# A Mamba scan with its carried state folded into the drive term, and time-step rows fetched in two parts

## Chip, cores and metric

One core of one Trainium2 chip. The metric is the device time of one execution in microseconds; three runs before the change gave 7946.76, 7952.61 and 7958.2, median 7952.61 us. The engines are named as in the profile: PE (TensorE), DVE (VectorE), ACT (ScalarE), POOL (GpSimd) and SP (SyncE, which here only issues DMAs).

## What is computed

Two layers with skips, on x of shape (4, 512, 64, 64): x = x + mamba_layer(group_norm(x)), then x = x + linear_attention(group_norm(x)). The change lies in the scan of the first layer. The 512 channels of each of the four images are cut into 4 chunks of 128; each chunk goes through the same Mamba block with 256 inner channels and 16 states, over a sequence of 4096 positions:

```python
dt = softplus(dbc[..., :8] @ dt_proj_w.T + dt_proj_b)
A = -jnp.exp(A_log)
def step(h, inp):
    dt_t, B_t, C_t, x_t = inp
    dA = jnp.exp(dt_t[:, :, None] * A)
    h = dA * h + (dt_t * x_t)[:, :, None] * B_t[:, None, :]
    y = jnp.einsum('bds,bs->bd', h, C_t)
    return (h, y)
_, ys = lax.scan(step, h0, ...)
y = (ys + xc * D_param) * silu(z)
```

Below, u is dt * x (here x is the block's convolved input), "drive" is u * B, and the state h at the end of one tile of positions is the start of the next tile.

## The kernel before

**Tiles and steps.** The 4096 positions are cut into 8 tiles of T = 512. A *step* is one (image b, tile t, chunk c), c innermost: 4 x 8 x 4 = 128 steps. So the same chunk's next tile comes four steps later, and its state waits in `st`. A step has 16 *slots*, numbered s = 0 to 15 (g counts slots over the whole loop, 2048 in all): two halves of the inner channels (e), in each four groups of states (q), in each two slots (jj) of two scans. So a step has 32 scans of 128x512. Partitions hold 4 states by 32 channels. Two slots, a *pair*, share one tile `h` of 128x4x512.

**What a slot does** (`slot`, lines 725 to 754):

- `drive(g + 2)` on POOL: the product of u and B, 128x1024, into a tile `bx` (three buffers), line 721;
- in even slots `b_row`, in odd slots `c_tail`: four small DMAs each, on SP's queue, that spread rows of B or of the last quarter of C over the partitions (line 688);
- two scans on DVE, line 739, each with `decay` for the scan three further on: ACT's exponential into one of three PSUM banks `dA` (line 713). A scan starts from the constant 0.0 in tile 0 and from a column of `st` in tiles 1 to 7;
- in even slots, between the two scans, DVE's product of the pair before with C's first 384 positions (`product`, line 759); `fold_states` follows it on PE (the sum over states into `y`);
- in odd slots, after the second scan, POOL's copy of the four last columns of `h` into `st` (line 750) and POOL's product of the last 128 positions with C, the *tail* (line 751).

PE's fold of a pair needs the tail; it frees one of the two `h` buffers for the pair after the next one.

**Between slots** the function `after` places the rest by slot number. That part is written out by hand, and each engine runs its instructions in the order written; the framework adds only the waits on data and buffers. What matters here: dt of the next step is made in slot 3 by ACT (two Softplus, line 620, with a table load before and after); in slot 4 POOL makes u next to it (line 628; the tile `both`, 128x2x2x512, tag `dt`, has one buffer); in slot 5 SP writes both to DRAM (line 631, one DMA each); in slot 9 SP fetches both back for the next step's first half, each over four groups of partitions: eight DMAs of 256 KB (`spread`, line 639). The second half is fetched in slot 1 of the step itself, eight DMAs again. Gates (POOL, line 781) come in slots 1 and 9, Silu with two table loads (ACT) in slot 10.

**Attention and the norms** of other tiles run in the same slots, mainly on PE and ACT, from the end of batch 0 on. After the last scan (7493.4 us into the span) the last image's attention runs alone.

**SP's queue** has all loads and stores of the loop, in order. An issue waits until the DMA issued eight places earlier has landed: over the trace no issue starts before that landing, and a fifth of them start within 0.2 us after it.

Of the kernel before, what the change touches and what calls it, by code (L numbers as in the profile page):

```python
# [24 lines left out]
def kernel(  # L25
# [196 lines left out]


    w_cv = const.tile([P, NTAP, DI], F32, tag="w_cv", name="w_cv")
    w_x = wk.tile([P, DI], F32, tag="bx", name="w_x", bufs=3)
    nc.scalar.dma_start(w_x, in_w[:, 0:DI])
    conv_bc = wk.tile([P, NTAP, DI], F32, tag="h", name="conv_bc", bufs=2)
    nc.scalar.dma_start(conv_bc, conv_w.partition_broadcast(P))
# [41 lines left out]


    bqk = const.tile([P, C], BF16, tag="bqk", name="bqk")
    b_qk = wk.tile([P, C], F32, tag="bx", name="b_qk", bufs=3)
    nc.vector.memset(b_qk, 0.0)
    for i in range(P // LANE):
        nc.scalar.dma_start(
# [290 lines left out]
    def shifted_end(f, name):  # L567
        mv = small.tile([P, NC, 2], F32, tag="mv", name=f"mv_{name}", bufs=4)
        for v in range(2):
            nc.vector.tensor_reduce(mv[:, :, v], f[("sum", "square")[v]], AX.X, ALU.add)  # L570
        nc.vector.tensor_scalar(mv, mv, 1.0 / L, None, ALU.mult)
        d2 = small.tile([P, NC], F32, tag="d2", name=f"d2_{name}")
        nc.vector.tensor_tensor(d2, mv[:, :, 0], mv[:, :, 0], ALU.mult)
        nc.vector.tensor_tensor(mv[:, :, 1], mv[:, :, 1], d2, ALU.subtract)
        nc.vector.tensor_tensor(mv[:, :, 0], mv[:, :, 0], f["mv"][:, :, 0], ALU.add)
        return mv
# [41 lines left out]
    def time_steps(f, nm):  # L618
        for e in range(NH):
            nc.scalar.activation(  # L620
                f["both"][:, 0, e, :], f["pt"][e], AF.Softplus, bias=dtb[:, e : e + 1]
            )

    def to_rows(f, v, nm):

        both = f["both"]
        if v:
            nc.gpsimd.tensor_tensor(f["both"][:, 1], f["both"][:, 0], f["xz"][:, 0], ALU.mult)  # L628
        d_rows = dram.tile([P, NH, T], F32, tag=f"d_rows{v}", name=f"d_rows{v}_{nm}")
        f["d_rows", v] = d_rows  # L630
        later(1, lambda: nc.sync.dma_start(d_rows, both[:, v]))

    def spread(f, e, nm):

        d = wk.tile([P, 2, NJ, T], F32, tag="d_all", name=f"d_all_{nm}_{e}")
        for v in range(2):
            src = f["d_rows", v].rearrange("(j i) e t -> i e j t", i=BLK)[:, e]
            for k in range(KS):
                nc.sync.dma_start(d[k * BLK : (k + 1) * BLK, v], src)  # L639
        f["d_all", e] = d  # L640

    def mixers(f, nm):

        pd = work_bank(f"pd_{nm}", 0)
        for e in range(NH):
            mm(pd, w_xp[:, e, :], f["xz"][:, 0, e, :], start=(e == 0), stop=(e == NH - 1))
        yield
        f["both"] = wk.tile([P, 2, NH, T], F32, tag="dt", name=f"dt_{nm}", bufs=1)  # L650
        dtr = f["dtr"] = f["both"][0 : 2 * LANE, 1, NH - 1, :]
# [28 lines left out]
        e, r = divmod(r, NQ * JJ)  # L680
        return n, e, *divmod(r, JJ)

    b_all, c_all, c_sb, dAs, bxs, hs, ys = {}, {}, {}, {}, {}, {}, {}

    def for_states(dst, rows_, q):

# [30 lines left out]
    def drive(g):  # L717

        n, e, q, jj = place(g)
        bxs[g] = wk.tile([P, 2, T], F32, tag="bx", name=f"bx_{g}", bufs=3)  # L720
        nc.gpsimd.tensor_tensor(  # L721
            bxs[g], fs[n]["d_all", e][:, 1, jj * 2 : jj * 2 + 2, :], bc(b_all[g // JJ], 2), ALU.mult
        )

    def slot(g, last, after):
        n, e, q, jj = place(g)
        b, t, c = steps[n]
        if g + 2 < last:
            drive(g + 2)
        if jj == 0:  # L730
            if g + 3 * JJ < last:
                b_row(g + 3 * JJ)
            hs[g // JJ] = wk.tile([P, NJ, T], F32, tag="h", name=f"h_{g}", bufs=2)
        elif g + 1 < last:
            c_tail(g + 1)
        h = hs[g // JJ]
        for i in range(2):
            j = jj * 2 + i
            nc.vector.tensor_tensor_scan(  # L739
                h[:, j, :], dAs.pop(2 * g + i), bxs[g][:, i, :],  # L740
                0.0 if t == 0 else st[:, c, e, q, j : j + 1], ALU.mult, ALU.add,
            )
# [5 lines left out]
        del bxs[g]  # L748
        if jj == JJ - 1:
            nc.gpsimd.tensor_copy(st[:, c, e, q, :], h[:, :, T - 1])  # L750
            nc.gpsimd.tensor_tensor(  # L751
                h[:, :, CUT:], h[:, :, CUT:], bc(c_sb.pop(g // JJ), NJ), ALU.mult
            )
# [52 lines left out]
    def attention(b, x1s, stats):  # L806
# [87 lines left out]

        kqn = wk.tile([P, NC, P], F32, tag="res", name=f"kqn_{b}", bufs=2)
        nc.gpsimd.memset(kqn, 0.0)
        nrm = small.tile([P, NC], F32, tag="nrm", name=f"nrm_{b}")
# [116 lines left out]
    def run(pieces):  # L1014
        for _ in pieces:
            pass
# [59 lines left out]
    c_tail(0)  # L1076
    time_banks(fs[0], names[0])
    time_steps(fs[0], names[0])
    for v in range(2):
        to_rows(fs[0], v, names[0])  # L1080
    spread(fs[0], 0, names[0])
    for g in range(JJ, 3 * JJ, JJ):
        b_row(g)
    c_row(0)
    for g in range(2):
        drive(g)
    run(step_inputs(1))
    silu(1)
    run(mixers(fs[1], names[1]))
# [4 lines left out]
    with tc.manual_schedule():  # L1094
        credit, seen, mix, held[0], held_x[0] = 0.0, work["mm"], iter(()), 0, 0
        for n, (b, t, c) in enumerate(steps):
# [10 lines left out]
            for s in range(SLOTS):  # L1107
                def after():
# [8 lines left out]
                        take_y(f, n, 0)  # L1117
                    if s < 2:
                        next(last_mix, None)
                    if s == 1:  # L1120
                        spread(f, 1, nm)
                        if before is not None:
                            gate(before, 1)
                    if s == 2 and nxt is not None:
                        time_banks(nxt, names[n + 1])
                    if s == 3 and nxt is not None:
# [7 lines left out]
                            add_to(late, leave(pb_, pt_))  # L1134
                    if s in (3, 5, 6, 7, 8, 9):
                        next(front, None)
                    if s == 4 and nxt is not None:
                        to_rows(nxt, 0, names[n + 1])
                        to_rows(nxt, 1, names[n + 1])
                    if s == 4 and before is not None:  # L1140
                        pb_, pt_, pc_ = steps[n - 1]
                        out_proj(before, xn[pb_, pt_], pc_, names[n - 1])
                    if s == 9:
                        gate(f, 0)
                        if nxt is not None:
                            spread(nxt, 0, names[n + 1])
                    if s == 10 and n + 2 < N:
                        silu(n + 2)
                        nc.scalar.preload_act_table_set("natural_log_exp_and_others")
# [90 lines left out]
```

## Time and profile before

| | |
|---|---|
| median of 3 runs | 7952.61 us |
| profiled execution | 7963.09 us, its span 7961.4 us |
| mean granted TensorE clock | 0.897 |
| busy: DVE, POOL | 6977.7 (88%), 6880.5 (86%) us |
| busy: PE, ACT | 6453.6 (81%), 5507.6 (69%) us |
| DMA | 1265.87 MB, mean 159 GB/s |
| loop of scans | 122.4 to 7493.4 us of the span |
| POOL copies into `st` | 1024, mean 204 ns, median 188 ns, 209.1 us busy |
| `d_all` fetches, `d_rows` writes, median to landing | 6.7 us (256 KB), 3.6 us (512 KB) |

Busy time is the union of an engine's instructions; an engine idles where it waits for another. A group of instructions is one line, engine and pair of tiles: its count, its busy time, the mean of one, and the idle time of the engine just before them with what ended most of it. Records of consecutive independent instructions overlap by some 0.05 us on POOL and 0.08 on DVE, so distances between starts tell throughput better than durations.

### The profile page before, as it was taken

The page shows a single profiled execution, that of the slowest core. Times are in us where ns is not written, and L with a number is a line of the kernel's source. Part 1 is how long each engine was busy: PE and PEld are TensorE (multiplying, and loading weights), DVE is VectorE, ACT ScalarE, POOL GpSimd, SP SyncE. Part 2 cuts the span into 40 slices and gives each one's busy share as a digit, 9 for nine tenths or more (in the row PEclk, how much of TensorE's full clock was granted, in tenths as well). Part 3 has the DMA queues.
Part 4 walks back from the last instruction along what each step waited for, and adds up shares of the span by engine and source line. Part 5 has one row for each costly group of instructions (what it writes and reads, how often), then busy time and mean ns, then how long its engine had stood idle before and what let it go on. Part 6 is the DMA issues. An engine that isn't in the chain of part 4 may idle for free.

```text
span 7961.4 us, 90563 instructions
## 1 busy us (share of the span) xinstructions
PE 6453.6 (81%) x24835; PEld 2120.0 (27%) x24880; DVE 6977.7 (88%) x5766; ACT 5507.6 (69%) x8321; POOL 6880.5 (86%) x4597
## 2 busy tenths in 40 slices
PE   5676777677789888888788888898688888888599
PEld 1121212112223222322222223332122332322144
DVE  5999999999999999989999999998999999988600
ACT  4667777777777777767777777677777777777421
POOL 4999999999999899989999899898999999889600
PEclk7888888888899999998899999899899999999799
DMA  5666666666666666777766666677666666676402
GB/s 154 167 168 166 151 155 159 160 155 167 169 179 162 151 163 159 174 189 175 174 155 171 171 157 161 155 185 189 156 167 163 161 161 159 145 194 180 112 32 90
DMA packets 829184, 1265.87 MB, mean 159 GB/s; under 512 B 183912, under 2 KB 317560, under 8 KB 816384
## 3 DMA queue, kind: packets, MB, share of 16 engines
q1 hardware_dynamic: 804736, 1222.32, 61.1%
q0 software_dynamic: 16896, 33.56, 2.4%
q10 hardware_dynamic: 7040, 4.20, 0.2%
q8 instruction: 195, 3.19, 0.2%
q14 instruction: 317, 2.60, 0.1%
HBM read 1052.78 MB, written 206.57 MB: 158 GB/s over the span
## 4 chain that ended last, share of the span: by engine, by line
DVE 33%; PE 21%; ACT 15%; DMA 12%; issue 8%; SPq 6%; POOL 6%; POOLq 0%; ACTq 0%; DVEq 0%
DVE h L739 22%; DVE h L759 9%; DMA d_all<-d_rows 7%; ACT dA L713 5%; PE pq L124 5%; POOL bx L721 4%; PE pc L124 4%; SPq L688 3%; PE y L124 3%; PE pr L124 3%; SPq L639 2%; DMA c_sb<-c_rows 2%; ACT xz L1048 2%; PE po L124 2%; ACT L1048 1%
## 5 line engine op out<-in xcount | busy, mean ns | idle before, releaser
L721 POOL TENSOR_TENSOR bx<-d_all,b_all 128x1024 f32<-128x1024 f32 x2048 | 4824.7, 2367 | 213.3 <-DVE h L739 195.1
L739 DVE TENSOR_TENSOR_SCAN h<-dA,st,bx 128x512 f32<-128x512 f32 x3584 | 4358.9, 1264 | 358.7 <-ACT dA L713 159.0
L713 ACT ACTIVATE dA<-d_all,a_t 128x512 f32<-128x512 f32 x4096 | 2752.9, 687 | 1568.5 <-DVE h L739 1521.8
L759 DVE TENSOR_TENSOR h<-h,c_all 128x1536 f32<-128x1536 f32 x1024 | 1767.5, 1726 | 0.1
L751 POOL TENSOR_TENSOR h<-h,c_sb 128x512 f32<-128x512 f32 x1024 | 1300.2, 1270 | 190.2 <-DMA c_sb<-c_rows 95.2
L124 PE MATMUL y<-h,fold 128*32 128x512 f32 x8192 | 1271.2, 696 | 71.6 <-POOL h L751 67.4
L124 PE MATMUL c_all<-parts,sel 128*128 128x384 bf16 x1024 | 369.9, 361 | 1123.3 <-DVE h L759 1121.7
L124 PE MATMUL pc<-xn,w_cv 128*128 128x512 f32 x2048 | 1045.7, 645 | 122.8 <-DVE xn L414 62.1
L124 PE MATMUL pq<-w_qk,xa 128*128 128x512 f32 x2048 | 965.5, 604 | 7.9 <-issue 5.3
L739 DVE TENSOR_TENSOR_SCAN h<-dA,bx 128x512 f32<-128x512 f32 x512 | 591.2, 1203 | 90.0 <-ACT dA L713 65.1
L124 PEld LDWEIGHTS <-sel 128*128 128x128 bf16 x1280 | 127.1, 99 | 1762.2 <-DVE h L759 1562.5
L124 PEld LDWEIGHTS pc<-xn,w_cv 128*128 128x128 f32 x2048 | 389.5, 201 | 747.1 <-issue 424.7
L124 PEld LDWEIGHTS pq<-w_qk,xa 128*128 128x128 f32 x2048 | 398.6, 196 | 439.6 <-issue 422.4
L124 PE MATMUL pr<-xb,m 128*128 128x512 f32 x1024 | 485.3, 612 | 7.5 <-DMA xb<-x 3.6
L124 PE MATMUL pp<-xn,w_pr 128*128 128x512 f32 x1024 | 477.7, 597 | 4.8 <-DVE xn L414 4.8
L124 PEld LDWEIGHTS y<-h,fold 128*32 128x32 f32 x8192 | 170.6, 114 | 644.0 <-issue 344.9
L124 PE MATMUL y<-xz,dg 32*32 32x512 f32 x2048 | 337.3, 734 | 0.0
L781 POOL TENSOR_TENSOR xz<-xz 128x512 f32<-128x512 f32 x256 | 325.7, 1272 | 9.2 <-ACT xz L778 9.2
L832 ACT ACTIVATE kq<-pq 128x512 f32<-128x512 f32 x256 | 150.5, 588 | 259.9 <-PE pq L124 259.2
L124 PE MATMUL pd<-xz,w_xp 128*128 128x512 f32 x512 | 323.4, 764 | 7.8 <-ACT xz L1048 7.8
L628 POOL TENSOR_TENSOR dt<-dt,xz 128x1024 f32<-128x1024 f32 x128 | 302.3, 2361 | 24.7 <-ACT dt L620 24.6
L124 PE MATMUL pz<-xn,w_z 128*128 128x512 f32 x512 | 275.4, 631 | 11.7 <-ACT xz L608 8.2
(179 smaller groups left out, 6034.1 us busy)
## 6 DMA issues: line engine op xcount, KB each, us to landing
d_all<-d_rows SPq DMA_DIRECT2D x2048, 256.0 KB, 6.7
b_all<-b_rows SPq DMA_DIRECT2D x4096, 64.0 KB, 2.2
d_rows<-dt SPq DMA_DIRECT2D x256, 512.0 KB, 3.6
c_sb<-c_rows SPq DMA_DIRECT2D x4096, 16.0 KB, 1.8
xs<-in_x_dram SPq DMA_DIRECT2D x32, 1024.0 KB, 6.3
xn<-in_x_dram SPq DMA_DIRECT2D x32, 1024.0 KB, 6.2
xr<-in_x_dram POOLq DMA_DIRECT2D x32, 1024.0 KB, 10.7
x<-xr SPq DMA_DIRECT2D x32, 1024.0 KB, 4.2
```

The costliest lines, as they stand in the source:

```text
L124: nc.tensor.matmul(out_, lhsT, rhs, **how)
L628: nc.gpsimd.tensor_tensor(f["both"][:, 1], f["both"][:, 0], f["xz"][:, 0], ALU.mult)
L639: nc.sync.dma_start(d[k * BLK : (k + 1) * BLK, v], src)
L688: nc.sync.dma_start(dst[k * BLK : (k + 1) * BLK, :], rows_[q * KS + k, :].partition_broadcast(BLK))
L713: nc.scalar.activation(dAs[k], fs[n]["d_all", e][:, 0, j, :], AF.Exp, scale=a_t[:, e, j, q : q + 1])
L721: nc.gpsimd.tensor_tensor(bxs[g], fs[n]["d_all", e][:, 1, jj * 2 : jj * 2 + 2, :], bc(b_all[g // JJ], 2), ALU.mult)
L739: nc.vector.tensor_tensor_scan(h[:, j, :], dAs.pop(2 * g + i), bxs[g][:, i, :], 0.0 if t == 0 else st[:, c, e, q, j : j + 1], ALU.mult, AL ...
L751: nc.gpsimd.tensor_tensor(h[:, :, CUT:], h[:, :, CUT:], bc(c_sb.pop(g // JJ), NJ), ALU.mult)
L759: nc.vector.tensor_tensor(own, own, bc(c_all.pop(g // JJ), NJ), ALU.mult)
L781: nc.gpsimd.tensor_tensor(f["xz"][:, 1, e, :], f["xz"][:, 1, e, :], f["xz"][:, 0, e, :], ALU.mult)
L832: nc.scalar.activation(qk[i], pq, AF.Relu)
L1048: nc.scalar.activation(fs[n]["xz"], fs[n]["xz"], AF.Silu)
```

## The change

All scans start from the constant 0.0. What the state of the tile before adds is added to the first column of `bx` instead: exp(dt_0 * A) * h_before, for 32 scans of a step, laid out in `carry` (128 x 2 x 4 x 4).

- In tiles 1 to 7, for each half: POOL multiplies A by dt's first position (`carry_over`), ACT takes the exponential (`carry_decay`), POOL multiplies by `st` (`carry_on`); then after the second product of every pair POOL adds the pair's four values to the four first columns of its two ring slots (`first`).
- `bx` becomes one constant tile of four slots, and a product is made three slots ahead, where it was two.
- The last columns of `h` go to `st` by ACT's copy right after the second scan, ahead of the next decay; in slot 11, after Silu, by POOL as before. They go there in tile 0 too.
- u overwrites dt in place: dt is written to DRAM in slot 5, u is made in slot 6 and written in slot 8. The tile has half its size.
- The fetches come in two parts of four DMAs: dt in slot 7 and u in slot 9 for the next step's first half, dt in slot 0 and u in slot 1 for the second.
- B's rows are fetched in odd slots, after C's, where they were fetched in even slots.
- Two set-up tiles and two small tags change their places.

```diff
     def to_rows(f, v, nm):
-        both = f["both"]
-        if v:
-            nc.gpsimd.tensor_tensor(f["both"][:, 1], f["both"][:, 0], f["xz"][:, 0], ALU.mult)
         d_rows = dram.tile([P, NH, T], F32, tag=f"d_rows{v}", name=f"d_rows{v}_{nm}")
         f["d_rows", v] = d_rows
-        later(1, lambda: nc.sync.dma_start(d_rows, both[:, v]))
+        nc.sync.dma_start(d_rows, f["dt"])
+
+    def times_input(f):
+        nc.gpsimd.tensor_tensor(f["dt"], f["dt"], f["xz"][:, 0], ALU.mult)
 
-    def spread(f, e, nm):
-        d = wk.tile([P, 2, NJ, T], F32, tag="d_all", name=f"d_all_{nm}_{e}")
-        for v in range(2):
-            src = f["d_rows", v].rearrange("(j i) e t -> i e j t", i=BLK)[:, e]
-            for k in range(KS):
-                nc.sync.dma_start(d[k * BLK : (k + 1) * BLK, v], src)
-        f["d_all", e] = d
+    def spread(f, e, v, nm):
+        if v == 0:
+            f["d_all", e] = wk.tile([P, 2, NJ, T], F32, tag="d_all", name=f"d_all_{nm}_{e}")
+        src = f["d_rows", v].rearrange("(j i) e t -> i e j t", i=BLK)[:, e]
+        for k in range(KS):
+            nc.sync.dma_start(f["d_all", e][k * BLK : (k + 1) * BLK, v], src)
...
+    RING, DRIVE = 4, 3
+    bx = const.tile([P, RING, 2, T], F32, tag="bx", name="bx")
+    carry = const.tile([P, NH, NJ, NQ], F32, tag="carry", name="carry")
...
     def drive(g):
         n, e, q, jj = place(g)
-        bxs[g] = wk.tile([P, 2, T], F32, tag="bx", name=f"bx_{g}", bufs=3)
         nc.gpsimd.tensor_tensor(
-            bxs[g], fs[n]["d_all", e][:, 1, jj * 2 : jj * 2 + 2, :], bc(b_all[g // JJ], 2), ALU.mult
+            bx[:, g % RING], fs[n]["d_all", e][:, 1, jj * 2 : jj * 2 + 2, :],
+            bc(b_all[g // JJ], 2), ALU.mult,
         )
+        if jj == JJ - 1 and steps[n][1]:
+            if q == 0:
+                carry_on(g)
+            r = (g - jj) % RING
+            first = bx[:, r : r + JJ, :, 0].rearrange("p r i -> p (r i)")
+            nc.gpsimd.tensor_tensor(first, first, carry[:, e, :, q], ALU.add)
+
+    def carry_over(g):
+        n, e, _, _ = place(g)
+        nc.gpsimd.tensor_tensor(
+            carry[:, e], a_t[:, e],
+            fs[n]["d_all", e][:, 0, :, 0].unsqueeze(2).to_broadcast([P, NJ, NQ]), ALU.mult,
+        )
+
+    def carry_decay(g):
+        _, e, _, _ = place(g)
+        nc.scalar.activation(carry[:, e], carry[:, e], AF.Exp)
+
+    def carry_on(g):
+        n, e, _, _ = place(g)
+        nc.gpsimd.tensor_tensor(
+            carry[:, e], carry[:, e], st[:, steps[n][2], e].rearrange("p q j -> p j q"), ALU.mult
+        )
+
+    def starts_half(g, last):
+        return g < last and g % (SLOTS // NH) == 0 and steps[g // SLOTS][1] > 0
+
+    def keep(g, h, copy):
+        n, e, q, _ = place(g)
+        copy(st[:, steps[n][2], e, q, :], h[:, :, T - 1])
 
     def slot(g, last, after):
         n, e, q, jj = place(g)
-        b, t, c = steps[n]
-        if g + 2 < last:
-            drive(g + 2)
+        if starts_half(g + DRIVE + 1, last):
+            carry_over(g + DRIVE + 1)
+        if g + DRIVE < last:
+            drive(g + DRIVE)
         if jj == 0:
-            if g + 3 * JJ < last:
-                b_row(g + 3 * JJ)
             hs[g // JJ] = wk.tile([P, NJ, T], F32, tag="h", name=f"h_{g}", bufs=2)
-        elif g + 1 < last:
-            c_tail(g + 1)
+        else:
+            if g + 1 < last:
+                c_tail(g + 1)
+            if g + 1 + 3 * JJ < last:
+                b_row(g + 1 + 3 * JJ)
...
             nc.vector.tensor_tensor_scan(
-                h[:, j, :], dAs.pop(2 * g + i), bxs[g][:, i, :],
-                0.0 if t == 0 else st[:, c, e, q, j : j + 1], ALU.mult, ALU.add,
+                h[:, j, :], dAs.pop(2 * g + i), bx[:, g % RING, i, :], 0.0, ALU.mult, ALU.add,
             )
+            if i == 1 and jj == JJ - 1 and g % SLOTS - 1 not in AWAY:
+                keep(g, h, nc.scalar.copy)
             if 2 * g + i + LEAD < 2 * last:
                 decay(2 * g + i + LEAD)
...
+        if starts_half(g + DRIVE, last):
+            carry_decay(g + DRIVE)
         if jj == JJ - 1:
-            nc.gpsimd.tensor_copy(st[:, c, e, q, :], h[:, :, T - 1])
+            if g % SLOTS - 1 in AWAY:
+                keep(g, h, nc.gpsimd.tensor_copy)
...
-                    if s == 1:
-                        spread(f, 1, nm)
-                        if before is not None:
-                            gate(before, 1)
+                    if s in (0, 1):
+                        spread(f, 1, s, nm)
+                    if s == 1 and before is not None:
+                        gate(before, 1)
...
-                    if s == 4 and nxt is not None:
-                        to_rows(nxt, 0, names[n + 1])
-                        to_rows(nxt, 1, names[n + 1])
+                    if s in (5, 8) and nxt is not None:
+                        to_rows(nxt, int(s == 8), names[n + 1])
+                    if s == 6 and nxt is not None:
+                        times_input(nxt)
...
+                    if s in (7, 9) and nxt is not None:
+                        spread(nxt, 0, int(s == 9), names[n + 1])
                     if s == 9:
                         gate(f, 0)
-                        if nxt is not None:
-                            spread(nxt, 0, names[n + 1])
```

More of the change, by code (lines that the diff above doesn't have):

```diff
@@ L224 @@
     w_cv = const.tile([P, NTAP, DI], F32, tag="w_cv", name="w_cv")
-    w_x = wk.tile([P, DI], F32, tag="bx", name="w_x", bufs=3)
+    w_x = wk.tile([P, DI], F32, tag="res", name="w_x", bufs=2)
     nc.scalar.dma_start(w_x, in_w[:, 0:DI])
@@ L272 @@
     bqk = const.tile([P, C], BF16, tag="bqk", name="bqk")
-    b_qk = wk.tile([P, C], F32, tag="bx", name="b_qk", bufs=3)
+    b_qk = wk.tile([P, C], F32, tag="res", name="b_qk", bufs=2)
     nc.vector.memset(b_qk, 0.0)
@@ L571, in shifted_end @@
         nc.vector.tensor_scalar(mv, mv, 1.0 / L, None, ALU.mult)
-        d2 = small.tile([P, NC], F32, tag="d2", name=f"d2_{name}")
+        d2 = small.tile([P, NC], F32, tag="d2", name=f"d2_{name}", bufs=1)
         nc.vector.tensor_tensor(d2, mv[:, :, 0], mv[:, :, 0], ALU.mult)
@@ L620, in time_steps @@
             nc.scalar.activation(
-                f["both"][:, 0, e, :], f["pt"][e], AF.Softplus, bias=dtb[:, e : e + 1]
+                f["dt"][:, e, :], f["pt"][e], AF.Softplus, bias=dtb[:, e : e + 1]
             )
     def to_rows(f, v, nm):
-        both = f["both"]
-        if v:
-            nc.gpsimd.tensor_tensor(f["both"][:, 1], f["both"][:, 0], f["xz"][:, 0], ALU.mult)
         d_rows = dram.tile([P, NH, T], F32, tag=f"d_rows{v}", name=f"d_rows{v}_{nm}")
         f["d_rows", v] = d_rows
-        later(1, lambda: nc.sync.dma_start(d_rows, both[:, v]))
-    def spread(f, e, nm):
-        d = wk.tile([P, 2, NJ, T], F32, tag="d_all", name=f"d_all_{nm}_{e}")
-        for v in range(2):
-            src = f["d_rows", v].rearrange("(j i) e t -> i e j t", i=BLK)[:, e]
-            for k in range(KS):
-                nc.sync.dma_start(d[k * BLK : (k + 1) * BLK, v], src)
-        f["d_all", e] = d
+        nc.sync.dma_start(d_rows, f["dt"])
[7 more added lines that the diff above has]
+            nc.sync.dma_start(f["d_all", e][k * BLK : (k + 1) * BLK, v], src)
     def mixers(f, nm):
@@ L649, in mixers @@
         yield
-        f["both"] = wk.tile([P, 2, NH, T], F32, tag="dt", name=f"dt_{nm}", bufs=1)
-        dtr = f["dtr"] = f["both"][0 : 2 * LANE, 1, NH - 1, :]
+        f["dt"] = wk.tile([P, NH, T], F32, tag="dt", name=f"dt_{nm}", bufs=1)
+        dtr = f["dtr"] = f["dt"][0 : 2 * LANE, NH - 1, :]
         nc.scalar.copy(dtr, pd[0 : 2 * LANE, :])
@@ L681, in place @@
         return n, e, *divmod(r, JJ)
-    b_all, c_all, c_sb, dAs, bxs, hs, ys = {}, {}, {}, {}, {}, {}, {}
+    b_all, c_all, c_sb, dAs, hs, ys = {}, {}, {}, {}, {}, {}
+    RING, DRIVE = 4, 3
+    bx = const.tile([P, RING, 2, T], F32, tag="bx", name="bx")
+    carry = const.tile([P, NH, NJ, NQ], F32, tag="carry", name="carry")
     def for_states(dst, rows_, q):
@@ L747, in slot @@
                 fold_states(g - 1, last)
-        del bxs[g]
+        if starts_half(g + DRIVE, last):
+            carry_decay(g + DRIVE)
         if jj == JJ - 1:
-            nc.gpsimd.tensor_copy(st[:, c, e, q, :], h[:, :, T - 1])
+            if g % SLOTS - 1 in AWAY:
+                keep(g, h, nc.gpsimd.tensor_copy)
             nc.gpsimd.tensor_tensor(
@@ L896, in attention @@
         nc.gpsimd.memset(kqn, 0.0)
-        nrm = small.tile([P, NC], F32, tag="nrm", name=f"nrm_{b}")
+        nrm = small.tile([P, NC], F32, tag="nrm", name=f"nrm_{b}", bufs=1)
         nc.vector.tensor_reduce(nrm, kq, AX.X, ALU.add)
@@ L1078 @@
     time_steps(fs[0], names[0])
-    for v in range(2):
-        to_rows(fs[0], v, names[0])
-    spread(fs[0], 0, names[0])
+    to_rows(fs[0], 0, names[0])
+    spread(fs[0], 0, 0, names[0])
+    times_input(fs[0])
+    to_rows(fs[0], 1, names[0])
+    spread(fs[0], 0, 1, names[0])
     for g in range(JJ, 3 * JJ, JJ):
@@ L1084 @@
     c_row(0)
-    for g in range(2):
+    for g in range(DRIVE):
         drive(g)
+    b_row(3 * JJ)
     run(step_inputs(1))
```

## Prediction

> **What bounds the kernel now.** I read the groups of instructions first. Two engines carry the loop, VectorE (DVE) with the scans of line 739 and GpSimd (POOL) with the products of line 721; ScalarE (ACT) and TensorE wait for them.
>
> ```profile
> L721 POOL TENSOR_TENSOR bx<-d_all,b_all 128x1024 f32<-128x1024 f32 x2048 | 4824.7, 2367 | 213.3 <-DVE h L739 195.1
> L739 DVE TENSOR_TENSOR_SCAN h<-dA,st,bx 128x512 f32<-128x512 f32 x3584 | 4358.9, 1264 | 358.7 <-ACT dA L713 159.0
> L751 POOL TENSOR_TENSOR h<-h,c_sb 128x512 f32<-128x512 f32 x1024 | 1300.2, 1270 | 190.2 <-DMA c_sb<-c_rows 95.2
> L739 DVE TENSOR_TENSOR_SCAN h<-dA,bx 128x512 f32<-128x512 f32 x512 | 591.2, 1203 | 90.0 <-ACT dA L713 65.1
> ```
>
> The reader is to see two prices for one scan: 1264 ns where it starts from a column of `st`, 1203 ns where it starts from the constant 0.0 (the 16 steps with t = 0).
>
> Then the busy times by stretch: the steps with t > 0 of batch 0, and of batches 1 to 3 (columns: length, then busy time of PE, PE's weight loads, DVE, ACT, POOL; clock, DMA share, GB/s).
>
> ```profile
> 338.40:1896.60 1558.20, 1114.28 (x4162) 303.61 (x4162) 1502.40 (x1188) 1134.54 (x1699) 1503.50 (x1003) 0.82 0.67 160
> 2124.80:3766.60 1641.80, 1415.00 (x5594) 478.63 (x5601) 1528.05 (x1247) 1207.93 (x1832) 1504.01 (x1004) 0.94 0.67 168
> 3995.00:5638.10 1643.10, 1416.16 (x5594) 480.18 (x5600) 1527.54 (x1246) 1207.89 (x1832) 1503.58 (x1004) 0.94 0.67 168
> 5865.70:7493.40 1627.70, 1387.35 (x5524) 460.23 (x5530) 1505.25 (x1208) 1178.33 (x1788) 1498.08 (x998) 0.93 0.66 165
> ```
>
> DVE and POOL are equally loaded everywhere: 1502 and 1504 of 1558 us in batch 0, 1528 and 1504 of 1642 in batch 1. Neither alone is the bound, and work moved from one to the other is not a gain by itself.
>
> Last the timeline around slots 4 to 6 of one step.
>
> ```profile
> 2374.59 4.16 SPq L688 DMA_DIRECT2D c_sb<-c_rows  x3
> ...
> 2380.67 0.21 POOL L750 COPY st<-h 128x4 f32<-128x4 f32 x1
> 2380.70 0.40 SPq L143 DMA_DIRECT2D xs<-in_x_dram  x1
> 2380.96 1.28 POOL L751 TENSOR_TENSOR h<-h,c_sb 128x512 f32<-128x512 f32 x1
> 2381.18 1.28 ACT L713 ACTIVATE dA<-d_all,a_t 128x512 f32<-128x512 f32 x2
> ...
> 2382.20 4.66 POOL L721 TENSOR_TENSOR bx<-d_all,b_all 128x1024 f32<-128x1024 f32 x2
> 2382.41 1.50 ACT L367 ACTIVATE xa<-xa,off_b,gr_b 128x512 f32<-128x512 f32 x2
> 2383.23 0.84 SPq L631 DMA_DIRECT2D d_rows<-dt  x2
> ```
>
> It shows what a small POOL operation costs in place: the copy starts at 2380.67 and the tail product that follows it at 2380.96, so 0.29 us, of which 0.08 is idle hand-over between two instructions on the same tile (0.26 in the step's quieter pairs). Unrelated POOL instructions overlap by about 0.05 instead. It also shows how late SP is: the write of dt and u to DRAM belongs to slot 5 and is issued at 2383.23, while POOL works on slots 6 and 7.
>
> **The change, part by part.**
>
> *Scans from zero.* 3584 scans lose 1264 - 1203 = 61 ns: 219 us off DVE, 54.7 per stretch above (896 scans). In the timeline four scans in a row take 4.80 us with t > 0 and 4.56 with t = 0, so it is throughput, not a longer record.
>
> *Copies of the last column.* Seven of the eight per step leave POOL for ACT: 7 x 128 = 896, at 0.26: -233 us of POOL. ACT gets 896 small copies; ACT's nearest rows are 189 ns (128x1 accumulator read) and 256 ns (128x32 exponential), so about +0.2 each. ACT is busy 1208 of 1643 us and its largest wait is 1521.8 us for the scans; the copy waits for the same scan that the following dA waits for, so it delays that dA by 0.2 us, and two scans and a product (1.2 + 1.2 + 1.7) lie before it is needed. What is late next is POOL: its tail product writes over the column, so it now waits for ACT. In the timeline above ACT is behind in slot 5: the copy would lie between the two dA that start at 2381.18, end near 2382.1, and hold the tail by 1.1 us. That is hidden wherever POOL is itself a microsecond late.
>
> *First columns.* 112 steps x 8 = 896 additions of 128x4 on POOL, by coincidence as many as the copies removed. The trace has none of the kind. Nearest is the 128x4 copy, 188 ns median; each reads what the instruction before it wrote. Low bound 0.14 (copy less overlap), high 0.36 (two hand-overs); I take 0.27, the copy's price in place: +242 us, bounds 125 to 323.
>
> *The carry itself.* Two products of 128x16 per half step, 4 x 112 = 448, nearest row the 128x12 copies (about 197 ns): 0.15 overlapped to 0.28 with hand-over; I take 0.18: +81 us (67 to 125). The 224 exponentials on ACT, 0.256 each, add 57 us that dA's waits cover.
>
> Sum on POOL: -233 + 242 + 81 = **+90 us**, bounds -41 to +215; per stretch -51 + 60 + 20 = +30. On DVE: **-219 us**.
>
> *Ring of four, three ahead.* The product for slot g+3 overwrites what slot g-1 read, as before with three buffers and two ahead. But the addition waits for the second of a pair, so the first slot of a pair still has two slots of lead; only the second gains one. Worth nothing on its own; at a low bound a loss where an early product holds the tail queued behind it, at most the wait POOL has for DVE there (195 us in all).
>
> *u in dt's place, and split fetches.* The DMAs are as many (256 writes, 2048 fetches of 256 KB). The eight fetches in a row at slots 1 and 9 hold SP now:
>
> ```profile
> SPq L688 <- DMA d_all<-d_rows: 1555.2, 1736, 3.9
> ```
>
> Four and four in slots 0 and 1 (7 and 9) start a slot earlier, so the C rows behind them should land earlier; POOL's 95.2 us of waiting for them is the most it can give, and I take half. Against it: u's product may not overwrite dt before dt's write has been read out, so POOL now waits for a DMA that SP issues. With its product queue up to the tail behind it, DVE waits next. Bounds per step: nothing, to what the timeline gives with SP as late as now: POOL would be ready after its first product, 2382.2 + 2.3 = 2384.5; the write issued at 2383.23 lands a median 3.6 us later, 2386.8: 2.3 us. I take 0.1, since SP's lateness in slots 3 to 6 comes from the eight fetches that are now spread out.
>
> *A rule that speaks against it.* In the first full window DVE and POOL are busy 193.82 and 197.27 of 200 us at once:
>
> ```profile
> 200.00:400.00 200.00, 130.39 (x491) 33.13 (x490) 193.82 (x162) 135.19 (x198) 197.27 (x133) 0.81 0.67 166
> ```
>
> So in these forms one does not stop the other, and the sum has no term for it. The Trainium skill (Perfetto Trace Analysis, Optimizing Scalar/DVE Operations) warns that moving work between DVE and GpSimd may not help, since they share a read port that one can lock. By that rule the 896 additions would come off DVE's time as well, 896 x 0.19 = 170 us of the 219, and the total would come out slower; the row above goes against it.
>
> **From work to time.** POOL in the four stretches, with 224 hand-overs of 0.08 (18 us) each, is occupied 1522, 1522, 1522, 1516 and idle 37, 120, 121, 112. After: 1552, 1552, 1552, 1546. DVE falls to about 1450 to 1473, so POOL sets the pace and what counts is how much of its idle time stays. In batch 0 some 29 us of it waits for DVE and 5 for C rows, in batch 2 81 and 25. DVE gets 85 us earlier relative to POOL in each, so I leave a third of the first and half of the second, keep the rest (3 and 14), and add 10 for the waits on ACT and for dt: 26, 64, 64, 60. The stretches become 1578, 1616, 1616, 1606: +20, -26, -27, -22, sum -55. The four t = 0 stretches (900.2 us) lose 16 x 7 x 0.26 = 29 us of POOL and nothing on DVE, which is busy 850 there: -12. Total -67 on a span of 7961.4. Around the span lie 1.7 us (7963.1 for that execution), and the median of the runs, 7952.6, is 10.5 under it: **7885 us**.
>
> **Rivals.**
> 1. *DVE's gain shows nearly whole* (0.13). For: POOL's largest wait is for DVE. Idle time of 5 and three times 25: stretches sum to 6282 against 6470.8, -189 - 12: 7750.
> 2. *Nothing measurable* (0.13). For: equal loads, and POOL gains 90. POOL's idle time falls by about its added work: 7937 to 7968.
> 3. *u's product waits for dt's write* (0.25). The mechanism above; it cancels the gain from 67/127 = 0.53 us per step, and at 1.6 us gives 7885 + 127 x 1.5 = 8075. For: the timeline above. Against: SP should be earlier.
> 4. *POOL's idle time stays, being due to others* (0.05): +30 x 4 - 12 = +108: 8060.
> 5. *The ring, now one tile, ties each scan to the newest product* (0.02): not what the change says. Every slot would be a product and two scans, 2.4 + 2.4 against 3.6: over 10,000. Against: `st` is one tile too, and scans do not wait for its latest copy (5.6 us in all).
>
> **Numbers.** The forecast, POOL-paced and faster, has 0.42; with rival 1 faster has 0.55, same 0.13, slower 0.32. A measurement here tells 0.2%, 16 us, from no change. Its own range is 7830 to 7936. The overall range goes to 7770 (rival 1, less than half) and 8040 (rival 3 at 1.3 us).
>
> **What would show it.** Scans of one group at about 1203 ns; additions near 0.19 us with 0.08 before them; POOL's busy time about 40 to 90 us up and its wait for scans down to a third; DVE's wait for POOL's products well above 78 us; the C row wait halved; u's product waiting for dt's write under 15 us in all. The prediction is wrong if that last wait is over 70 us, or tails wait for ACT's copies by more than 70, or POOL's idle time doesn't fall.

## The result, and the profile after

| | before | after |
|---|---|---|
| median of runs, us | 7954.3 | 8078.71 (8065.92 to 8089.73) |
| ratio | 1 | 1.0157, 95% interval 1.0139 to 1.0175 |
| profiled execution's span, us | 7961.4 | 8075.6 |
| busy DVE, POOL, us | 6977.7, 6880.5 | 6784.5, 6996.1 |
| loop of scans, us of the span | 122.4 to 7493.4 | 124.0 to 7608.1 |
| `c_sb`, `d_rows`, `d_all`, median to landing, us | 1.8, 3.6, 6.7 | 4.0, 6.2, 5.1 |

The kernel became slower by 1.6%, about 124 us. The spans of the profiled executions differ by 114 us, and 113 of these lie in the loop, between the first scan's start and the last one's end.

First the groups of instructions of the changed kernel (busy time, mean ns of one, idle time before them and what ended most of it).

```profile
L775 DVE TENSOR_TENSOR_SCAN h<-dA,bx 128x512 f32<-128x512 f32 x4096 | 4753.9, 1207 | 737.4 <-POOL bx L731 262.6
L722 POOL TENSOR_TENSOR bx<-d_all,b_all 128x1024 f32<-128x1024 f32 x2048 | 4860.1, 2376 | 171.9 <-DMA c_sb<-c_rows 73.0
L790 POOL TENSOR_TENSOR h<-h,c_sb 128x512 f32<-128x512 f32 x1024 | 1318.3, 1287 | 160.5 <-ACT st L757 98.9
```

Every scan is a short one now, 1207 ns. But the idle time before the scans has grown from 449 us (358.7 + 90.0) to 737.4, and what ends the largest part of it, 262.6 us, is POOL's addition.

The same view for POOL alone has the new small operations.

```profile
L731 POOL TENSOR_TENSOR bx<-bx,carry 128x4 f32<-128x4 f32 x896 | 186.3, 208 | 70.2
L747 POOL TENSOR_TENSOR carry<-carry,st 128x16 f32<-128x16 f32 x224 | 52.6, 235 | 0.0
```

An addition is 208 ns, and the 70.2 us of idle time before the 896 are 78 ns each. The view names no engine that ends them: they are the hand-over from the product whose output the addition reads. With L736 (49.6 us) the carry occupies POOL for 359 us.

Then the busy times of the four stretches with t > 0, cut at the same scans as before (length, PE, weight loads, DVE, ACT, POOL; clock, DMA share, GB/s).

```profile
346.11:1942.97 1596.86, 1128.90 (x4162) 309.75 (x4162) 1456.84 (x1188) 1156.71 (x1950) 1535.44 (x1140) 0.82 0.64 156
2178.81:3836.48 1657.67, 1427.40 (x5593) 481.23 (x5600) 1477.13 (x1247) 1231.73 (x2082) 1538.40 (x1141) 0.93 0.66 167
4069.81:5727.54 1657.73, 1425.42 (x5593) 483.29 (x5600) 1477.69 (x1246) 1231.59 (x2082) 1538.34 (x1141) 0.93 0.66 167
5958.80:7608.09 1649.29, 1388.00 (x5522) 462.85 (x5528) 1458.00 (x1208) 1201.17 (x2039) 1527.91 (x1134) 0.93 0.65 163
```

They are longer by 39, 16, 15 and 22 us. DVE is down by 46 to 51 us in each, POOL up by 30 to 35, and POOL's idle time is 61, 119, 119 and 121 us, where it was 55, 138, 140 and 130: hardly less. The four t = 0 stretches between them, which have neither carry nor shorter scans, grew from 900.4 to 922.6 us.

Last the waits of POOL (us in total, times, longest), before and then after.

```profile
POOL bx L721 <- DVE h L739: 195.1, 290, 6.6
POOL h L751 <- DMA c_sb<-c_rows: 95.2, 63, 6.6
POOL st L750 <- DVE h L739: 78.9, 79, 5.4
```

```profile
POOL h L790 <- ACT st L757: 98.9, 77, 5.5
POOL dt L631 <- DMA d_rows<-dt: 98.1, 53, 25.6
POOL bx L722 <- DMA c_sb<-c_rows: 73.0, 94, 4.0
...
POOL bx L722 <- DVE h L775: 31.4, 25, 6.8
```

POOL's waits for scans, 274 us before (195.1 for its products, 78.9 for its copies), are down to 31. Three others have taken their place, and two of them are for transfers. One wait of 25.6 us for dt's write lies ahead of the loop; inside it there are 72.5.

The third line of the second view names the C rows, but a product doesn't read those; by the order on SP's queue it is another transfer. Of the product's idle time, 100.6 us lie before the product for slot 8 (made in slot 5), 0.79 us in a mean step, and that product is the first to read the second half's u. One such case in the timeline, POOL first, then SP:

```profile
3681.31 0.21 POOL L731 TENSOR_TENSOR bx<-bx,carry 128x4 f32<-128x4 f32 x1
3684.87 2.36 POOL L722 TENSOR_TENSOR bx<-d_all,b_all 128x1024 f32<-128x1024 f32 x1 [3.35 <-DMA c_sb<-c_rows]
```

```profile
3673.55 3.31 SPq L690 DMA_DIRECT2D b_all<-b_rows  x4
3676.91 2.81 SPq L639 DMA_DIRECT2D d_all<-d_rows  x4
```

The four fetches of u are issued from 3676.91 to 3679.72; a median 5.1 us after that is 3684.8, and POOL starts at 3684.87. They stand behind the B rows, and that is where the following timeline leads: SP at the turn of one step to its slot 5, and POOL at the same time.

```profile
4187.94 1.75 SPq L690 DMA_DIRECT2D c_sb<-c_rows  x4
4190.26 3.27 SPq L690 DMA_DIRECT2D b_all<-b_rows  x4
...
4201.78 1.76 SPq L690 DMA_DIRECT2D c_sb<-c_rows  x4
4204.27 1.70 SPq L690 DMA_DIRECT2D b_all<-b_rows  x4
4206.07 0.37 SPq L628 DMA_DIRECT2D d_rows<-dt  x1
```

```profile
4187.87 2.37 POOL L722 TENSOR_TENSOR bx<-d_all,b_all 128x1024 f32<-128x1024 f32 x1
...
4201.87 2.37 POOL L722 TENSOR_TENSOR bx<-d_all,b_all 128x1024 f32<-128x1024 f32 x1
4204.33 0.21 POOL L731 TENSOR_TENSOR bx<-bx,carry 128x4 f32<-128x4 f32 x1
```

The C rows of a slot go out, and then SP stands still until POOL's product has ended: 4187.87 + 2.37 = 4190.24, B rows at 4190.26; 4201.87 + 2.37 = 4204.24, B rows at 4204.27. The write of dt stands behind them. (Among SP's waits these stand under the addition that follows such a product on POOL, L731: 321.6 us.) The code says why. In odd slot g the row of the pair that begins at slot g + 7 overwrites the buffer that `drive(g + 2)` reads, which POOL was given only in slot g - 1. In an even slot, with products three ahead, a row waits for `drive(g + 1)`, which POOL was given in slot g - 2. So SP, which is in order, is held to POOL's newest product, and everything behind it with it. The distance alone is not the difference to the kernel before: there, two ahead, the even slot's row also waits for a product given in slot g - 1, and SP's wait for POOL's products is 79.7 us. In the odd slot the C rows come first, and they have just waited for the tail of slot g - 2; the product that the B rows then need is the next one on POOL after this tail.

### The profile page after: what moved, and what is told of

Same layout as the page of the kernel before. It is cut to its first block, busy times and chain, and to the rows that moved or that the text cites. A ratio compares the mean times of both kernels' runs of the same rounds, so it can differ in the third digit from the quotient of the medians.

```text
span 8075.6 us, 92769 instructions
## 1 busy us (share of the span) xinstructions
PE 6498.0 (80%) x24835; PEld 2138.4 (26%) x24880; DVE 6784.5 (84%) x5766; ACT 5612.2 (69%) x9441; POOL 6996.1 (87%) x5045
## 4 chain that ended last, share of the span: by engine, by line
PE 15%; DVE 12%; DMA 9%; ACT 5%; POOL 4%; SPq 3%; issue 3%; POOLq 0%; DVEq 0%; ACTq 0%
DVE h L775 8%; PE pq L124 4%; DVE h L798 3%; DMA d_all<-d_rows 3%; POOL bx L722 3%; PE y L124 2%; PE pr L124 2%; DMA c_sb<-c_rows 2%; PE pc L124 2%; SPq L690 2%; ACT dA L715 2%; POOL h L790 1%; SPq L639 1%; DMA b_all<-b_rows 1%; PE po L124 1%
## 5 line engine op out<-in xcount | busy, mean ns | idle before, releaser
L775 DVE TENSOR_TENSOR_SCAN h<-dA,bx 128x512 f32<-128x512 f32 x4096 | 4753.9, 1207 | 737.4 <-POOL bx L731 262.6
L715 ACT ACTIVATE dA<-d_all,a_t 128x512 f32<-128x512 f32 x4096 | 2781.6, 687 | 1226.6 <-DVE h L775 1180.7
L790 POOL TENSOR_TENSOR h<-h,c_sb 128x512 f32<-128x512 f32 x1024 | 1318.3, 1287 | 160.5 <-ACT st L757 98.9
L631 POOL TENSOR_TENSOR dt<-dt,xz 128x1024 f32<-128x1024 f32 x128 | 301.8, 2358 | 112.1 <-DMA d_rows<-dt 98.1
L817 ACT COPY xz<-y 128x512 f32<-128x512 f32 x256 | 149.3, 583 | 274.5 <-PE y L124 273.0
L124 PE MATMUL pz<-xn,w_z 128*128 128x512 f32 x512 | 310.2, 703 | 8.9 <-ACT xz L608 5.6
```

What stands on the lines that cost most here:

```text
L124: nc.tensor.matmul(out_, lhsT, rhs, **how)
L631: nc.gpsimd.tensor_tensor(f["dt"], f["dt"], f["xz"][:, 0], ALU.mult)
L715: nc.scalar.activation(dAs[k], fs[n]["d_all", e][:, 0, j, :], AF.Exp, scale=a_t[:, e, j, q : q + 1])
L775: nc.vector.tensor_tensor_scan(h[:, j, :], dAs.pop(2 * g + i), bx[:, g % RING, i, :], 0.0, ALU.mult, ALU.add,)
L790: nc.gpsimd.tensor_tensor(h[:, :, CUT:], h[:, :, CUT:], bc(c_sb.pop(g // JJ), NJ), ALU.mult)
L817: nc.scalar.copy(f["xz"][:, 0, e, :], ys.pop((n, e)))
```

## Experiments

Ratios are to the kernel before on the same chip, with 95% intervals; a difference in us is a difference of ratios times 7954 us. The scans from zero, the copies and the carry come first, then the transfers.

### Scans from zero alone

Every scan of the kernel before starts from 0.0; the state of the tile before is left out.

```diff
-                0.0 if t == 0 else st[:, c, e, q, j : j + 1], ALU.mult, ALU.add,
+                0.0, ALU.mult, ALU.add,
```

> The kernel before with every scan started from the constant 0.0; the state of the tile before is left out. It takes 3584 x 61 ns = 219 us off DVE and nothing else. POOL sets the pace (theory 1): POOL's 274 us of waiting for scans can shrink at most, and its other idle time stays, so 30 to 130 us less than before. DVE's work counts in full (theory 2): about 200 us less. Both engines wait for third parties, ACT and PE (theory 3): under 30 us less.

Measured: 7887.19 us, 0.9907 [0.9892, 0.9922], -74 us. Nothing is added to POOL here, and still only a third of DVE's 219 us shows. POOL's waits for scans fall from 274 to 175 us, its wait for C rows rises from 95.2 to 124.1, and DVE's wait for POOL's products from 78 to 136. POOL's idle time in the four stretches falls from 462 to 389 us, by 73: that is the gain, and in this kernel all that DVE's lead is worth.

### Copies on ACT alone

```diff
+            if i == 1 and jj == JJ - 1 and g % SLOTS - 1 not in AWAY:
+                nc.scalar.copy(st[:, c, e, q, :], h[:, :, T - 1])
...
-            nc.gpsimd.tensor_copy(st[:, c, e, q, :], h[:, :, T - 1])
+            if g % SLOTS - 1 in AWAY:
+                nc.gpsimd.tensor_copy(st[:, c, e, q, :], h[:, :, T - 1])
```

> The kernel before with seven of the eight state copies per step moved from POOL to ACT, as in the change, and nothing else. Theory 1 (POOL sets the pace): 896 x 0.26 = 233 us of POOL work goes, about 100 us of waiting for ACT's copies comes, so 50 to 130 us less than before. The rival: the tail's wait for ACT eats the whole gain, 0 to 50 us slower, since in the trace of before the tails would have come no earlier on average.

Measured: 7952.72 us, 0.9994 [0.9984, 1.0003]: nothing. POOL's waits show where most of its relief of 233 us went:

```profile
POOL h L754 <- ACT st L744: 184.4, 215, 5.6
```

The tail product now waits for ACT's copy, 215 times, 0.86 us each. In 172 of them, 158 us, the copy follows an exponential of line 713 on ACT with no idle time between: ACT is in order too and has other work ahead of it. The tails' wait for C rows grows as well, from 95.2 to 143.2 us.

### After without the carry

The additions, the products and the exponentials of the carried state are gone, and with them the state that goes from tile to tile.

```diff
-        if jj == JJ - 1 and steps[n][1]:
+        if False:
...
-        return g < last and g % (SLOTS // NH) == 0 and steps[g // SLOTS][1] > 0
+        return False
```

> The changed kernel without the additions to first columns, the two small products and the exponential per half (the carried state is left out of the scans); copies, ring and fetches as in the change. POOL loses 186 us of additions with 70 us of hand-over and 102 us of small products, 358 in all. Theory 1: 250 to 360 us less than the changed kernel, so 7720 to 7830. Rival (the waits for dt's write, u's fetch and ACT's copies set the loss, some 100 us each): POOL waits longer where it works less, and under 150 us is gained.

Measured: 7990.86 us, 1.0041 [1.0026, 1.0056], 92 us under the changed kernel. POOL has 359 us less to do, and a quarter of it shows: the wait for dt's write grows from 98.1 to 145.8 us, the products' waits under the names of C and B rows from 100 to 198. Without its added work POOL only reaches the late transfers sooner. It is also still slower than before, with all that the carry costs taken away: the rest of the loss had to be elsewhere.

### Earlier write and earlier fetches

```diff
+    spread(fs[0], 1, 0, names[0])
...
-                    if s in (0, 1):
-                        spread(f, 1, s, nm)
+                    if s == 0:
+                        spread(f, 1, 1, nm)
+                    if s == SLOTS - 1 and nxt is not None:
+                        spread(nxt, 1, 0, names[n + 1])
...
-                    if s in (5, 8) and nxt is not None:
+                    if s in (4, 8) and nxt is not None:
```

> The changed kernel with dt's write issued in slot 4 instead of 5, and the fetches for the second half one slot earlier (dt in slot 15 of the step before, u in slot 0). POOL's wait for dt's write (98 us) and the first product of the second half's wait for u (about 100 us, 0.79 per step before that product) should go. If these waits are part of the loss: 80 to 200 us less than the changed kernel, so 7880 to 8000. If POOL only waits there instead of waiting for scans later: under 40 us less.

Measured: 8099.15 us, 1.0183 [1.0166, 1.02]: no gain (21 us more than the changed kernel, with intervals that overlap). Both waits that it aimed at went (dt's write 98.1 to 28.1 us, all but the one ahead of the loop; the product of slot 8 from 0.79 to 0.04 us a step), and the tails' wait for C rows rose from 20.2 to 170.0. Moving these transfers in SP's queue moved the wait.

### U in dt's place and split fetches, in the kernel before

This takes `to_rows`, `times_input` and `spread` of the change into the kernel before, with their slots, and nothing else:

```diff
-                    if s == 4 and nxt is not None:
-                        to_rows(nxt, 0, names[n + 1])
-                        to_rows(nxt, 1, names[n + 1])
+                    if s in (5, 8) and nxt is not None:
+                        to_rows(nxt, int(s == 8), names[n + 1])
+                    if s == 6 and nxt is not None:
+                        times_input(nxt)
```

> The kernel before with only the new handling of dt and u: u made in dt's place in slot 6, dt written in slot 5 and u in slot 8, fetches in two parts (slots 7 and 9, 0 and 1). Ring of three, two ahead, scans from the saved state and POOL's copies stay. So far the parts give -69 (scans from zero), -4 (copies to ACT) and about +88 (carry work on POOL), sum +15, and the change gave +122, so about +104 us belong to the fetches or to the ring. Theory A (fetches: POOL waits for dt's write and for u's second half): 70 to 130 us slower than before. Theory B (the ring and B's rows behind C's in odd slots): within 25 us of before.

Measured: 8002.83 us, 1.0068 [1.0053, 1.0083], +54 us, although scans, copies and ring are those of before.

### The ring on top of it

To the last one are added the ring of four, products three slots ahead, and B's rows in odd slots; scans still start from `st`, POOL still copies (an excerpt; the ring itself and the set-up tiles that change their places with it are as in the change):

```diff
-        if g + 2 < last:
-            drive(g + 2)
+        if g + DRIVE < last:
+            drive(g + DRIVE)
         if jj == 0:
-            if g + 3 * JJ < last:
-                b_row(g + 3 * JJ)
...
+            if g + 1 + 3 * JJ < last:
+                b_row(g + 1 + 3 * JJ)
```

> The same with the ring of four, products three ahead, and B's rows fetched in odd slots; scans still start from the saved state, copies on POOL. Theory A: as the run before it, within 25 us. Theory B: 70 to 130 us slower than the run before it, because SP waits for POOL's newest products before it can fetch B's rows, and all its later DMAs come late.

Measured: 8064.19 us, 1.0142 [1.0125, 1.0159]: 59 us more. POOL's wait for dt's write is 121.5 us here, its products' waits for transfers 145.1 (89.4 and 55.7), where the kernel of the last section had 100.5 and 13.6.

### After with B's rows in even slots

```diff
         if jj == 0:
+            if g and g + 3 * JJ < last:
+                b_row(g + 3 * JJ)
...
-            if g + 1 + 3 * JJ < last:
-                b_row(g + 1 + 3 * JJ)
```

> The changed kernel with B's rows fetched in even slots again. If the order of SP's queue in odd slots (C's rows, which wait for POOL's tail, then B's rows, which wait for POOL's product) makes dt's write and u's fetch late, POOL's waits for them (98 and about 100 us) shrink and it is 50 to 150 us faster than the changed kernel. Otherwise within 25 us.

Measured: 7978.75 us, 1.0033 [1.002, 1.0046], 99 us under the changed kernel. In SP's waits, of the changed kernel and then of this one:

```profile
SPq L690 <- POOL bx L731: 321.6, 362, 2.1
```

```profile
SPq L690 <- POOL bx L731: 85.2, 136, 1.8
```

And POOL's waits here:

```profile
POOL dt L631 <- DMA d_rows<-dt: 34.5, 9, 25.6
POOL bx L722 <- DMA c_sb<-c_rows: 34.4, 52, 4.1
```

SP's wait under this name falls to a quarter. It is the place of the B rows that made dt's write and u's fetch late: both of POOL's waits for them fall, 98.1 to 34.5 and 73.0 to 34.4, though neither transfer was moved. The t = 0 stretches are back at 905.3 us.

### B's rows in even slots without the rest

The same edit on the kernel of the ring (*The ring on top of it*).

> The run with the new fetches and the ring of four, three ahead (scans from the saved state, copies on POOL; 115 us slower than before), with B's rows back in even slots. If B's rows in odd slots are what the ring costs (100 us in the changed kernel), 7950 to 7990, at or under the 8003 of the new fetches alone. If the ring itself costs, over 8030.

Measured: 7967.48 us, 1.001 [1.0001, 1.0019], 105 us under that kernel. So the place of the B rows costs the same with `st` scans and without a carry, and the ring with its third slot ahead, set free of it, is worth 46 us (1.001 against 1.0068).

These kernels also price the exchange of DVE's time for POOL's directly. From the kernel of the ring to the changed one only scans from zero, the copies on ACT and the carry are added: 1.0142 to 1.0157, +12 us. With B's rows in even slots the same three make 1.001 to 1.0033, +18 us. So they are no gain even where the queue is not held up.

### Split fetches alone

The kernel before with u beside dt as it was, and only the fetches in two parts.

```diff
-                    if s == 1:
-                        spread(f, 1, nm)
+                    if s in (0, 1):
+                        spread(f, 1, nm, (s,))
...
+                    if s in (7, 9) and nxt is not None:
+                        spread(nxt, 0, names[n + 1], (int(s == 9),))
                     if s == 9:
                         gate(f, 0)
-                        if nxt is not None:
-                            spread(nxt, 0, names[n + 1])
```

> The kernel before with the fetches in two parts (slots 7 and 9, 0 and 1), but u still made beside dt in slot 4 and both written in slot 5. Against the run with u in dt's place (54 us slower than before) it takes away POOL's wait for dt's write. If that wait is the loss: within 20 us of before, or faster by up to 50 us, since POOL's 95 us of waiting for C's rows shrink. If the split itself is the loss: 30 to 60 us slower than before.

Measured: 7929.1 us, 0.9952 [0.9939, 0.9966]: -38 us by the ratio, -27 by the medians (one of its five runs, 7907.21, lies apart). The tails' wait for C rows falls from 95.2 to 59.2 us. This version is faster than the kernel before and the changed one. Against it, u in dt's place costs 92 us (1.0068 - 0.9952; 81 by the medians).

### The write of dt one slot earlier

Two kernels: the changed one with B's rows in even slots, and the kernel before with u in place and split fetches, both with the write in slot 4.

```diff
-                    if s in (5, 8) and nxt is not None:
+                    if s in (4, 8) and nxt is not None:
```

> The changed kernel with B's rows in even slots (30 us slower than before) and dt's write issued in slot 4 instead of 5. POOL's last 8 us of waiting for that write in the loop go, and SP comes earlier to what follows: 7930 to 7980. Faster than before only if the waits for dt's write and u's fetch were still part of it; the earlier run that moved the write and the fetch moved POOL's wait to C's rows, and by that 7980 or more.

> The kernel before with u made in dt's place and the fetches in two parts (e5_before_fetch), and with the write of dt placed in slot 4 instead of slot 5, so that it is issued some slots before u's product in slot 6 asks for it. E5_before_fetch stood at 1.0068 to before, e9_before_split, which has the same fetches with u beside dt, at 0.9952. If the 81 us between them are GpSimd's wait for dt's write (100.5 us in e5_before_fetch), that wait falls to under 30 us and the ratio to 0.996 to 0.999. If the wait only moves, to the fetch of u's second half or to the C rows, the ratio stays at 1.004 to 1.008 and another wait of GpSimd grows by 50 us or more.

Measured: 7975.76 us, 1.0025 [1.0015, 1.0035], for the first: 6 us under the same kernel with the write in slot 5, within both intervals; its wait for the write was 34.5 us, of which 25.6 lie ahead of the loop. And 7948.63 us, 1.0005 [0.9996, 1.0015], for the second, 50 us under the same kernel with the write in slot 5. Its wait for the write, with the write in slot 5 and then in slot 4:

```profile
POOL dt L631 <- DMA d_rows<-dt: 100.5, 48, 25.4
```

```profile
POOL dt L631 <- DMA d_rows<-dt: 31.9, 9, 25.3
```

So of the 92 us for u in dt's place, about 50 go with that wait, which fell by 69. The other 42 stayed (31 by the medians): the ratio came to lie between the two that were expected. Their cause stays open, and their size is uncertain too, as the spans of the two profiled executions, taken on two chips, are only 12 us apart (7939.6 and 7928.0).

### The additions on DVE

DVE had time to spare, so the additions went there, ahead of each pair's first scan.

```diff
-            nc.gpsimd.tensor_tensor(first, first, carry[:, e, :, q], ALU.add)
...
+        if jj == 0 and steps[n][1]:
+            add_first(g)
```

(`add_first` is the same addition on `nc.vector`.)

> The changed kernel with the 896 additions to first columns on DVE instead of POOL, just before the pair's first scan. POOL loses 186 us of work and 70 us of hand-over, DVE gains 896 x 0.1 to 0.25 = 90 to 220 us. Leaving out all of the carry work (358 us of POOL) gained 88 us, so by proportion the additions on POOL cost 60 us; if POOL's work counts at that rate and DVE's at 69/219, the sum is 0 to -30 us against the changed kernel. If a hand-over from addition to scan on DVE costs as much as on POOL: slower, up to +40.

Measured: 8502.49 us, 1.0696 [1.068, 1.0712], +429 us on the changed kernel. The addition's group:

```profile
L735 DVE TENSOR_TENSOR bx<-bx,carry 128x4 f32<-128x4 f32 x896 | 751.2, 838 | 57.1 <-POOL bx L722 44.4
```

Four values a partition take 838 ns in the mean, between 133 and 5920. Two of them in the timeline, DVE first and then POOL:

```profile
4000.25 0.36 DVE L735 TENSOR_TENSOR bx<-bx,carry 128x4 f32<-128x4 f32 x1
...
4021.41 1.90 DVE L735 TENSOR_TENSOR bx<-bx,carry 128x4 f32<-128x4 f32 x1
```

```profile
3998.24 2.35 POOL L722 TENSOR_TENSOR bx<-d_all,b_all 128x1024 f32<-128x1024 f32 x1 [4.30 <-DMA d_all<-d_rows]
...
4018.61 4.67 POOL L722 TENSOR_TENSOR bx<-d_all,b_all 128x1024 f32<-128x1024 f32 x2
```

The first ends at 4000.61, POOL's product at 4000.59; the second at 4023.31, POOL's products at 4023.28. All 393 additions over 400 ns started while POOL was running and, but for the outer 5% at either side, end 19 to 34 ns after an instruction of POOL's; none of the 896 lies wholly inside one. They aren't slow; they stand still until POOL's instruction is over.

## Why the prediction was wrong

The forecast was -67 us on the span and 7885; the span grew by 114. By its own steps, first those that held.

**The prices.** Scans of one group at 1203 ns were foretold and came at 1207; additions of "0.27, the copy's price in place" took 0.208 + 0.078 = 0.286; the two products of the carry, 0.18, took 0.228. The occupied time of POOL in the stretches was put at 1552, 1552, 1552, 1546; it is 1553, 1556, 1556, 1545 (busy time and 224 hand-overs of 78 ns). The sum of work was right to 8 us over four stretches. POOL's busy time over the whole span rose by 116 us, though, where 40 to 90 were expected.

**The idle time, the step that failed.** The forecast needed POOL's idle time to shrink: "I leave a third of the first and half of the second, keep the rest (3 and 14), and add 10 for the waits on ACT and for dt: 26, 64, 64, 60." (The first are its waits for DVE, the second those for C rows.) Without the hand-overs it is 44, 102, 102 and 104: 352 us where 214 were forecast. These 138 us, the 8 above, and the t = 0 stretches (+22 for a forecast of -12) make up 180 of the 181 us between forecast and span. Three parts of that step fell:

- *DVE's lead was taken for too much.* The forecast took 176 us off POOL's idle time in all. With the scans shortened and nothing else changed, it fell by 73 (*Scans from zero alone*).
- *The copies were a transfer of the bound, not relief.* That the tail may wait for ACT was written down, "hidden wherever POOL is itself a microsecond late", and left without a term beyond that 10. It gave back all of the 233 us in the kernel before, and 98.9 us of POOL's time in the changed one.
- *SP was assumed to get earlier* ("SP should be earlier", "SP's lateness in slots 3 to 6 comes from the eight fetches that are now spread out"). The split does that, and is worth 38 us by itself. But the diff also moves B's rows from even slots to odd ones, behind C's, and the working has no term for that: under the ring it has "Worth nothing on its own", and under the fetches "The DMAs are as many". Each queue that a moved step passes should have been asked what the step waits for in its new place. It waits for POOL's newest product, and it costs 99 us in the changed kernel and 105 in the one without carry.

By part, as ratios times 7954 us: scans from zero -74, copies -5, the carry's work +92, split fetches -38, u in dt's place +92, ring and third slot ahead -46, B's rows in odd slots +105. The sum is +126, the change measured +125. So the parts add up, though each was taken in another surrounding, and the two for the split and for u in dt's place rest on the ratio of the split kernel, 11 us from its medians. The exchange of DVE's time for POOL's, which the forecast was built on, is worth about +13 by this sum (+12 and +18 directly); the transfers and the ring, which it took as a side matter, about +113.

**The C rows.** Half of 95.2 us was expected to go; the tail's wait for them fell to 20.2. But the queue's lateness came out at u's fetch instead, which the prediction didn't look at.

**The rivals.** "U's product waits for dt's write" gave 8075 and the time is 8078.7, but that is a coincidence of the sum: at 1.6 us a step it needed about 200 us of that wait, and the loop has 72.5. "POOL's idle time stays, being due to others", 8060 with a chance of 0.05, comes nearest to what the profile shows: idle 462 us before and 421 after, with scans replaced as the cause by copies, dt's write and u's fetch. The ring as one tile does not tie scans to the newest product: three-ahead with even rows gains. Two of the three signs that the prediction set against itself are there: u's wait for dt's write is 98.1 us, 72.5 of it in the loop (bound 70), the tails' wait for ACT 98.9 (bound 70). The third, that POOL's idle time doesn't fall, is not: it fell, by 40 us.

**The rule that speaks against moving work between DVE and GpSimd** was set aside by the row in which both are busy 193.82 and 197.27 of 200 us at once. For the change as it is that stands: scans went to 1207 ns beside POOL's additions. For another form it does not, as the last section shows.

## What to carry to other kernels

In a kernel with in-order queues, price a moved DMA by what it waits for in its new place and by what stands behind it, before counting bytes or instructions: here 32 small transfers a step, moved by one slot, cost more than the 219 us taken off the busiest engine gave. Where two engines are equally loaded, expect only a part of what is taken off one (here a third), and time moved from one to a third engine may come back whole as a wait for it. Change a fetch plan by itself first: of the parts that were put into the kernel before one at a time and keep its result, the split alone was a gain.

## What the runs showed of the hardware

A small VectorE addition of two operands in SBUF that starts beside a GpSimd instruction stands until that one is over, and ends some 20 to 30 ns after it (the last experiment). The kernel before has it as well, in its timeline:

```profile
4574.37 2.33 POOL L721 TENSOR_TENSOR bx<-d_all,b_all 128x1024 f32<-128x1024 f32 x1
4574.43 2.31 DVE L361 TENSOR_TENSOR off_a<-ngm_a,gr_a 128x4 f32<-128x4 f32 x1 [1.07 <-POOL gr_a L357]
...
7555.36 0.16 DVE L361 TENSOR_TENSOR off_b<-ngm_b,gr_b 128x4 f32<-128x4 f32 x1 [1.16 <-POOL gr_b L357]
```

The same 128x4 product takes 2.31 us when POOL's product began 0.06 us earlier, and 0.16 us with POOL idle. A scan, whose `dA` is in PSUM and whose `bx` is in SBUF, runs at 1.2 us beside the same products. This row could have been read before any run; it prices additions on DVE at POOL's remaining time, not at 0.1 to 0.25 us.

The Trainium skill (SBUF — State Buffer, section "SBUF: two separate sides") has the rule that fits: VectorE and GpSimd share a pair of ports as an exclusive lock, held for a whole instruction, which a VectorE instruction with two SBUF inputs needs against a GpSimd instruction that reads SBUF. The 838 ns mean against 133 ns at the least, and 2.31 against 0.16 us, agree with it.

One thing stays open: some products of line 722 take over 2.5 us, 73 after and 31 before, and more (167) where only the copies went to ACT. It is 15 us of POOL's time before and 35 after, and no run here shows why.
